# Head norm of a Taylor attention: sums for two groups at once, roots copied across partitions, values normed in place

## The chip, the cores and the metric

One core of one Trainium2 chip. The metric is the device time of one execution in microseconds (us). The engines are TensorE (PE; its weight loads are listed as PEld), VectorE (DVE), ScalarE (ACT), GpSimd (POOL) and SyncE (SP), which issues all of the DMA transfers of this kernel.

## The reference

The input x has 8 sequences (batches) of 512 tokens with 128 features. Two blocks are applied, each with a layer norm before, a layer norm after and a residual:

```
x = x + layernorm(taylor_attention(layernorm(x)))
x = x + layernorm(six_layer_transformer(layernorm(x)))
```

The first block is the one that changes. Its attention has 16 heads; a query or key has 16 features, a value has 64. The weight of a pair of tokens is a Taylor series of the exponential, which equals 0.5 * ((1 + q.k/4)^2 + 1), with a causal mask and no softmax. Behind it each head is normed on its own:

```
A   = tril(1 + s + s*s/2),  s = q.k/4
y   = A @ v                                            # per head, 512 x 64
y   = y * rsqrt(mean(y*y over 64) + 1e-5) * g_weight   # the head norm
out = concat(heads) @ Wo.T
```

The second block has six layers of local attention (window 32) and a gated feed-forward. It is unchanged, and it takes most of the time.

## The kernel before

The attention stage runs over groups of four heads: NQ = 4 groups in a batch, NG = 32 groups in all. Values are held transposed, with the 64 features of two heads in the 128 partitions and the 512 tokens along the row, so a group has a tile `yT` of 128 x 2 x 512, whose two halves hold two heads each.

A group takes three steps (`STEPS`), by blocks of keys: block 0, block 1, and blocks 2 and 3 together. `slot(k)` writes the order of PE for one step: `squares(k)` (scores `sc`, squared on ACT to `am`, masked on DVE at L283, which the text calls the keep), the head norm of an earlier group, the projections of the next group (`project_qk` in the second step, `project_v` in the third), the work of the neighbouring batches, and `weigh(k - 2)` (`y`, the weighted values, accumulated in PSUM). PE follows this order as written (`manual_schedule`); the order on the other engines is set by a scheduler, within the data dependencies. All engines are in order.

At the end of a group `weigh` lets DVE add the column sums `vs` to `y` and write `yT` (L308), and ACT square it to `ysq` (L313). The PSUM tile `y` has one buffer, so the next group's first `y` product waits for `yT`. Two slots after a group has ended, `head_norm(G)` computes the norm: PE multiplies `ysq` by `same` (128 x 128, ones in two 64 x 64 blocks), so that each partition gets the sum of its own head (L321); ACT takes the logarithm (L322) and exp(-0.5 * log) (L324), which gives the inverse root `rs` in each partition; DVE multiplies `yT`, the weight `gw` and `rs` to `yn` (L326). `attn_out(b)` multiplies the eight `yn` halves of a batch by Wo (`po`, L336), in the second group of the next batch, third step; a layer norm, a residual and a store of `x1` follow. The PSUM tiles of the tag `tr` (two buffers) serve `qk`, `vv`, `ms` and `po` in turn; the copies `tv` (L252) free those of `vv`.

The last pieces of this stage lie beside the first steps of the transformer: `head_norm(NG - 1)` at t = 0, and `attn_out(B - 1)` at t = 1.

Of the kernel before, what the change touches and what calls it, by code (L numbers as in the profile page):

```python
# [8 lines left out]
F32 = mybir.dt.float32  # L9
BF16 = mybir.dt.bfloat16  # L10
AF = mybir.ActivationFunctionType
ALU = mybir.AluOpType
# [3 lines left out]
P = 128  # L16
# [3 lines left out]
HD = 64  # L20
W = 32
# [7 lines left out]
def sandwich_kernel(ctx: ExitStack, tc: tile.TileContext, ins: dict, out: bass.AP):  # L29
    nc = tc.nc  # L30
    x_d = ins["L0_attn_hidden_states"]
    B, N, _ = x_d.shape
    NB = N // P
# [5 lines left out]
    NCH = len(CH)  # L39

    const = ctx.enter_context(tc.tile_pool(name="const", bufs=1))
# [23 lines left out]
    gw = vec[:, NV : NV + 1]  # L65
# [16 lines left out]
    tables, exps, divisions, copies, pcopies, maxima = [], [], [], [], [], []  # L82
# [12 lines left out]
    def issue_behind(later, earlier):  # L95
        tc.add_manual_dep(
            later.ins, earlier.ins.name,
            mybir.DependencyInfo(mybir.DependencyClass.NoSync, mybir.DependencyReason.DATA),
            reason="order on an engine",
        )  # L100
# [37 lines left out]
    psum = ctx.enter_context(tc.tile_pool(name="psum", bufs=2, space=PSUM))  # L138
    wl = ctx.enter_context(tc.tile_pool(name="wl", bufs=2))
    f2 = ctx.enter_context(tc.tile_pool(name="f2", bufs=2))  # L140
    f3 = ctx.enter_context(tc.tile_pool(name="f3", bufs=3))
    f1 = ctx.enter_context(tc.tile_pool(name="f1", bufs=1))
# [3 lines left out]
    NQ = H // 4  # L146
# [4 lines left out]
    def load_x(b):  # L151
        t = f2.tile([P, NP, W + P], F32, tag="kT", name=f"xin_{b}")
        xin[b] = t.rearrange("p a b -> p (a b)")[:, : NB * DM].rearrange("p (n d) -> p n d", d=DM)
        nc.sync.dma_start(xin[b], x_d[b].rearrange("(n p) d -> p n d", p=P))


    tw = wl.tile([P, 3, 2, 512], F32, tag="wqkv", name="tw")
    a_w = ins["attn_w"].rearrange("p (t s c) -> p t s c", t=3, s=2)
    nc.sync.dma_start(tw[:, 0], a_w[:, 0])
    load_x(0)  # L160
    nc.sync.dma_start(tw[:, 1], a_w[:, 1])
    nc.sync.dma_start(tw[:, 2], a_w[:, 2])
    nc.sync.dma_start(vec, ins["vectors"])
# [8 lines left out]
        out=keep, in_=keep, compare_op=ALU.is_ge, fill=0.0, base=0, pattern=[[1, P]], channel_multiplier=-1,  # L172
    )

    same = const.tile([P, P], F32, tag="same", name="same")
    nc.vector.memset(same, 0.0)
    for a in range(2):
        nc.vector.memset(same[HD * a : HD * (a + 1), HD * a : HD * (a + 1)], 1.0)
    eps4 = const.tile([P, 1], F32, tag="eps4", name="eps4")
    nc.vector.memset(eps4, 4.0 * EPS)  # L180

# [12 lines left out]
    for qd in range(4):  # L194
        r = slice(qd * W, (qd + 1) * W)
# [5 lines left out]
    NG = NQ * B  # L201
    bt = [dict() for _ in range(B)]
    gr = [dict() for _ in range(NG)]

    def norm_in(b):
        if b + 1 < B:
            load_x(b + 1)
        bt[b]["xl"] = xl = f1.tile([P, NB, DM], F32, tag="xn", name=f"xl_{b}")
        layer_norm(f2, xl, xin.pop(b), NB, by_log=True)
# [24 lines left out]
    def project_qk(G):  # L234
        b, g = divmod(G, NQ)
        gr[G]["qk"] = qk = f2.tile([P, 2, N], F32, tag="pe", name=f"tqk_{G}")
        for s in range(2):
            ps = psum.tile([P, N], F32, tag="tr", name="qk")
            nc.tensor.matmul(ps, wqk[:, s, g * P : (g + 1) * P], bt[b]["xlT"], start=True, stop=True)  # L239
            nc.scalar.copy(qk[:, s], ps)  # L240
# [48 lines left out]
    def weigh(k):  # L289

        G, s = steps[k]
        b, g = divmod(G, NQ)
        if s == 0:
            gr[G]["y"] = psum.tile([P, 2, N], F32, tag="s", name="y", bufs=1)
        y, v = gr[G]["y"], gr[G]["v"]
        am, places = gr[G].pop(("am", s))
        for m, o, n in places:
            for h in range(4):
                r = slice(HD * (h % 2), HD * (h % 2 + 1))
                nc.tensor.matmul(  # L300
                    y[r, h // 2, m * P :], v[:, m, h * HD : (h + 1) * HD], am[:, h, o : o + n],
                    start=(m == 0), stop=(m == NB - 1), skip_group_check=True,
                )
        if s == len(STEPS) - 1:
            yT = f2.tile([P, 2, NB, P], F32, tag="sq", name="yT")
            with tc.high_priority():
                for i in range(2):
                    nc.vector.tensor_tensor(  # L308
                        yT[:, i], y[:, i].rearrange("p (n m) -> p n m", m=P),
                        bt[b]["vs"][:, 2 * g + i, :].unsqueeze(2).to_broadcast([P, NB, P]), ALU.add,  # L310
                    )
            ysq = f2.tile([P, 2, N], F32, tag="t1", name="ysq")
            nc.scalar.activation(ysq, yT.rearrange("p a n m -> p a (n m)"), AF.Square)  # L313
            gr[G]["yT"], gr[G]["ysq"] = yT, ysq

    def head_norm(G):
        yT, ysq = gr[G].pop("yT"), gr[G].pop("ysq")
        rs = f2.tile([P, 2, N], F32, tag="t2", name="rs")
        for i in range(2):
            ps = psum.tile([P, N], F32, tag="tr", name="ms")  # L320
            nc.tensor.matmul(ps, same, ysq[:, i], start=True, stop=True)  # L321
            ln = nc.scalar.activation(rs[:, i], ps, AF.Ln, bias=eps4, scale=1.0 / HD)  # L322
            issue_behind(ln, tables[-1])
        exps.append(nc.scalar.activation(rs, rs, AF.Exp, scale=-0.5))  # L324
        gr[G]["yn"] = yn = f1.tile([P, 2, N], F32, tag=("qT", "pT", "on", "oT")[G % NQ], name="yn")
        nc.vector.scalar_tensor_tensor(  # L326
            yn.rearrange("p a n -> p (a n)"), yT.rearrange("p a n m -> p (a n m)"), gw,
            rs.rearrange("p a n -> p (a n)"), ALU.mult, ALU.mult,
        )

    def attn_out(b):

# [28 lines left out]
    def slot(k):  # L361

        G, ph = divmod(k, len(STEPS))
        b, g = divmod(G, NQ)
        if k < len(steps):
            squares(k)
        if ph == 0 and 0 <= G - 2 < NG:
            head_norm(G - 2)
        if ph == 1 and G + 1 < NG:
            project_qk(G + 1)  # L370
        if ph == 2 and G + 1 < NG:
            project_v(G + 1)
        if g == 0 and ph == 1 and b + 1 < B:
            norm_in(b + 1)
        if g == 1 and ph == 0 and b + 1 < B:
            in_by_features(b + 1)
        if g == 1 and ph == 1 and b + 1 < B:
            sums_before(b + 1)
        if g == 1 and ph == 2 and b >= 1 and k < len(steps):
            attn_out(b - 1)  # L380
        if g == 2 and ph == 2 and b >= 1 and k < len(steps):
            to_state(b - 1)
        if 0 <= k - 2 < len(steps):
            weigh(k - 2)
# [333 lines left out]
    def at(t, lag, step, *args, ends=False):  # L718
        if 0 <= t - lag < len(units) and (not ends or units[t - lag]["j"] == NB - 1):
            step(units[t - lag], *args)  # L720
# [3 lines left out]
    with tc.manual_schedule(engines={mybir.EngineType.PE}):  # L724
        norm_in(0)
        in_by_features(0)
        project_qk(0)
        project_v(0)
        sums_before(0)
        layers[0] = load_layer(0)  # L730
        for k in range(len(steps) + 2):
            slot(k)
        for t in range(len(units) + 7):
            if t < len(units):
                u = units[t]
                if u["l"] not in layers:
                    layers[u["l"]] = load_layer(u["l"])
                u["L"] = layers[u["l"]]


            gelus = 0 <= t - 5 < len(units) and units[t - 5]["j"] == NB - 1
            at(t, 0, proj, 0)
            at(t, 0, proj, 1)


            if t % NB == 1 and NB < t <= len(units) - NB * (B - 1):
                nc.tensor.addr_align(128, offset=IN_STEP)
            at(t, 2, by_keys)
            if gelus:
                gelu_only()  # L750
            at(t, 3, out_project)

            if t == 0:
                head_norm(NG - 1)
            if t == 1:
                attn_out(B - 1)
            at(t, 1, by_features, 0)
            at(t, 2, weigh_values)
            at(t, 1, by_features, 4, 0)
            at(t, 0, values)  # L760
            if t == 3:
                to_state(B - 1)
            at(t, 0, sum_squares, 0)
            at(t, 0, sum_squares, 1)
            if not gelus:
                at(t, 0, unit_length)
            at(t, 1, by_features, 4, 1)
            at(t, 0, spread)
            at(t, 3, feed_norm, ends=True)
            at(t, 4, feed_first, ends=True)  # L770
            at(t, 5, feed_middle, ends=True)
            if gelus:
                at(t, 0, unit_length)
            at(t, 6, feed_last, ends=True)
            at(t, 1, scores)
            at(t, 3, feed_normed, ends=True)
            at(t, 2, out_by_features)
# [91 lines left out]
```

## Time and profile before

| | |
|---|---|
| median of 3 runs | 3826.05 us |
| lowest and highest | 3818.64 and 3838.03 us |
| profiled execution, its own time | 3825.62 us |
| its span, first to last instruction | 3823.9 us |
| mean granted TensorE clock | 0.994 |
| PE busy in the span | 3703.6 us |
| DVE, ACT, POOL busy | 2794.7, 2662.9, 1842.6 us |
| stretch 100 to 500 us (attention): PE busy | 395.69 of 400 us |

A line of a group reads: line of the kernel, engine, operation, out<-in by the names of the tiles, the part of the array (for PE: rows * columns), shapes, count | busy time, mean ns of one | idle time of the engine just before, and what ended it. A float32 product is issued as two PE instructions, so counts on PE are twice those of the code. A line of a timeline has the start in us, the length, and the same names. In a table of stretches the DMA share is the mean busy share of the core's 16 DMA engines, and GB/s is what they moved.

### The profile page before, as it was taken

How to read it: one execution, taken by the hardware profiler on the slowest of the kernel's cores; microseconds unless marked ns; L12 is line 12 of the kernel's file. 1: busy time of each engine (PE TensorE's matmuls, PEld its weight loads, DVE VectorE, ACT ScalarE, POOL GpSimd, SP SyncE). 2: the span in 40 equal slices, each digit the busy share in tenths (PEclk: the TensorE clock that was granted, in tenths of full speed). 3: DMA queues.
4: the chain of work that ended last, by engine and by line, in shares of the span. 5: the costliest groups of instructions: out<-in, count | busy, mean ns of one | idle time of the engine just before them, and what ended most of it. 6: DMA issues, size and time to landing. Idle time of an engine off the chain costs nothing.

```text
span 3823.9 us, 152697 instructions
## 1 busy us (share of the span) xinstructions
PE 3703.6 (97%) x65600; PEld 2456.2 (64%) x65600; DVE 2794.7 (73%) x4308; ACT 2662.9 (70%) x6750; POOL 1842.6 (48%) x1311
## 2 busy tenths in 40 slices
PE   8999999999999999999999999999999999989997
PEld 4545556666666666666666666666666666666664
DVE  4555567787877778787777778777777878777774
ACT  5565557777777777777777777777777777767665
POOL 0000025555555555555555655555555555555552
PEclk9999999999999999999999999999999999999998
DMA  2000012222232222322222322223222222222221
GB/s 82 17 9 12 6 51 72 60 67 62 73 79 69 66 58 66 81 73 62 67 66 58 88 72 67 57 67 82 71 65 65 67 58 65 65 67 69 64 67 32
DMA packets 153219, 233.66 MB, mean 61 GB/s; under 512 B 32622, under 2 KB 53356, under 8 KB 151788
## 3 DMA queue, kind: packets, MB, share of 16 engines
q1 hardware_dynamic: 152556, 223.89, 22.8%
q8 instruction: 530, 8.68, 0.9%
q14 instruction: 133, 1.09, 0.1%
HBM read 24.54 MB, written 4.19 MB: 8 GB/s over the span
## 4 chain that ended last, share of the span: by engine, by line
PE 95%; issue 2%; ACT 2%; DVE 1%; POOL 0%; DMA 0%; POOLq 0%; SPq 0%; DVEq 0%; ACTq 0%
PE tr L79 20%; PE mm L439 17%; PE py L627 9%; PE mm L497 9%; PE po L598 8%; PE sp L558 8%; PE y L300 4%; PE mm L652 3%; PE mm L654 3%; PE py L687 3%; PE sc L270 3%; PE sp L551 2%; PE vv L248 2%; PE qk L239 1%; PE po L336 1%
## 5 line engine op out<-in xcount | busy, mean ns | idle before, releaser
L470 POOL TENSOR_TENSOR qk<-t,t 128x1024 f32<-128x1024 f32 x384 | 909.9, 2370 | 679.3 <-DVE t L454 405.3
L486 POOL TENSOR_TENSOR qk<-qk,ss 128x1024 f32<-128x1024 f32 x384 | 722.2, 1902 | 16.0
L439 PE MATMUL mm<-wqkv,state 128*128 128x512 f32 x1536 | 698.4, 597 | 2.6 <-ACT v L502 2.6
L447 DVE TENSOR_TENSOR t<-mm,tab 128x512 f32<-128x512 f32 x768 | 498.6, 671 | 239.5 <-PE mm L439 239.5
L570 ACT ACTIVATE pe<-sp,mx 128x64 f32<-128x64 f32 x3072 | 652.1, 381 | 2.3 <-DVE mx L566 2.3
L462 ACT ACTIVATE sq<-mm 128x512 f32<-128x512 f32 x768 | 421.3, 607 | 118.6 <-DVE t L454 114.0
L454 DVE TENSOR_TENSOR t<-mm,tab 128x1024 f32<-128x1024 f32 x384 | 468.4, 1220 | 5.9
L439 PEld LDWEIGHTS mm<-wqkv,state 128*128 128x128 f32 x1536 | 273.7, 191 | 289.6 <-issue 242.2
L473 DVE TENSOR_REDUCE ss<-sq 128x16 f32<-128x1024 f32 x384 | 448.6, 1209 | 0.7 <-ACT sq L462 0.6
L79 PE MATMUL tr<-ident,qk 128*128 128x128 f32 x3072 | 440.7, 276 | 1.8 <-ACT qT L536 0.8
L536 ACT COPY kT<-tr 128x512 f32<-128x512 f32 x384 | 225.6, 587 | 299.6 <-PE tr L79 299.4
L79 PEld LDWEIGHTS tr<-ident,qk 128*128 128x128 f32 x3072 | 351.0, 141 | 120.7 <-issue 100.8
L627 PE MATMUL py<-oT,wo 128*128 128x128 f32 x3072 | 377.4, 276 | 0.5 <-ACT oT L620 0.5
L627 PEld LDWEIGHTS py<-oT,wo 128*128 128x128 f32 x3072 | 364.5, 194 | 0.7 <-ACT oT L620 0.7
L497 PE MATMUL mm<-wqkv,state 128*128 128x512 f32 x768 | 363.1, 595 | 0.3 <-ACT sq L462 0.3
L620 ACT COPY oT<-tr 128x512 f32<-128x512 f32 x384 | 206.8, 589 | 221.5 <-PE tr L79 218.9
L598 PE MATMUL po<-v,pT 64*32 64x64 f32 x24576 | 301.9, 225 | 56.0 <-PE tr L79 49.1
L598 PEld LDWEIGHTS po<-v,pT 64*32 64x32 f32 x24576 | 274.2, 105 | 98.0 <-PE tr L79 88.5
L566 DVE TENSOR_REDUCE mx<-sp 128x16 f32<-128x1024 f32 x192 | 235.1, 1225 | 104.2 <-PE sp L558 104.2
L558 PE MATMUL sp<-kT,qT 64*32 64x64 f32 x24576 | 304.7, 226 | 6.4 <-issue 6.4
L558 PEld LDWEIGHTS sp<-kT,qT 64*32 64x32 f32 x24576 | 270.6, 105 | 62.5 <-issue 60.0
L606 DVE TENSOR_TENSOR on<-po,su 128x1024 f32<-128x1024 f32 x192 | 235.2, 1225 | 96.8 <-PE po L598 96.8
(114 smaller groups left out, 5082.8 us busy)
## 6 DMA issues: line engine op xcount, KB each, us to landing
v<-v SPq DMA_DIRECT2D x1152, 128.0 KB
v<-v SPq DMA_DIRECT2D x672, 64.0 KB
wqkv<-in_L_ffn_Wqkv_dram SPq DMA_DIRECT2D x6, 1536.0 KB
wo<-in_L_ffn_Wo_dram SPq DMA_DIRECT2D x6, 512.0 KB
xin<-_attn_hidden_states_dram SPq DMA_DIRECT2D x8, 256.0 KB
xr<-_attn_hidden_states_dram SPq DMA_DIRECT2D x8, 256.0 KB
x<-xr SPq DMA_DIRECT2D x8, 256.0 KB
xr<-x SPq DMA_DIRECT2D x8, 256.0 KB
```

Of the source, the lines that this page charges most:

```text
L79: nc.tensor.transpose(ps[:cols, :rows], src, ident[:rows, :rows])
L439: nc.tensor.matmul(ps[:, a].rearrange("p h d -> p (h d)"), lhs, wqkv[:, s, a, :], start=True, stop=True)
L447: nc.vector.tensor_tensor(t2[:, a], ps[:, 1 - a], tab[:, 2 * s + 1, j, HF * a : HF * (a + 1)].unsqueeze(1).to_broadcast([P, H, HF]), ALU.mult,
L454: nc.vector.tensor_tensor(t1, ps, tab[:, 2 * s, j, :].rearrange("p (a d) -> p a d", a=2).unsqueeze(2) .to_broadcast([P, 2, H, HF]), ALU.mult,)
L470: nc.gpsimd.tensor_tensor(qk[:, s].rearrange("p h a d -> p a h d"), t1, t2, ALU.add)
L473: su = nc.vector.tensor_reduce(u["ss"][:, s], u["sq", s].rearrange("p h a d -> p h (a d)"), AX.X, ALU.add)
L486: nc.gpsimd.tensor_tensor(t, t, ss[:, i, :].unsqueeze(2).to_broadcast([P, H, HD]), ALU.mult)
L497: nc.tensor.matmul(ps[:, p, :], lhs, L["wqkv"][:, 2, p, :], start=True, stop=True)
L558: nc.tensor.matmul(sp[W * w : W * (w + 1), p, pair, :], qT[HD * p : HD * (p + 1), pair, W * w : W * (w + 1)], kT[HD * p : HD * (p + 1), pa ...
L570: ex = nc.scalar.activation(pe[:, pair, p, :], sp[:, p, pair, :], AF.Exp, bias=mx[:, p, pair : pair + 1])
L598: nc.tensor.matmul(po[W * w : W * (w + 1), p, pair, :], pT[r, pair, W * w : W * (w + 1)], v2[r, w, HD * pair : HD * (pair + 1)], start=Tru ...
L627: nc.tensor.matmul(py, L["wo"][:, c, :], oT[:, c, :], start=(c == 0), stop=(c == NP - 1))
```

## The change

`head_norm` is called for two groups at once, in every second group, with the first of the two as its argument. The constant `same` becomes `of`, 128 x 32, with ones of one head in the even columns and of the other in the odd columns. Four products, one for each half of the two groups, write 32 partitions each of one PSUM tile `ps`: partition 32c + a holds the sum of head a of half c. ACT takes one logarithm and one exponential of 128 x 512, into a tile `rt` (tag `gT`). The eight rows that matter, one for each head, are then copied to the 64 partitions of their heads in `rs` by eight DMAs from SP, each with a source that is repeated 64 times. DVE multiplies in place: `yT` is both input and output, and is also what `attn_out` reads. `yT` now takes its buffer in turn from six places: the four single-buffer tags that `yn` had and the two buffers of `sq`.

The last call at t = 0 is for the last two groups. Apart from the head norm, the load of the first batch's x is issued ahead of the first third of the attention weights, where it was second.

```diff
     tw = wl.tile([P, 3, 2, 512], F32, tag="wqkv", name="tw")
     a_w = ins["attn_w"].rearrange("p (t s c) -> p t s c", t=3, s=2)
+    load_x(0)
     nc.sync.dma_start(tw[:, 0], a_w[:, 0])
-    load_x(0)
     nc.sync.dma_start(tw[:, 1], a_w[:, 1])
...
-    same = const.tile([P, P], F32, tag="same", name="same")
-    nc.vector.memset(same, 0.0)
+    of = const.tile([P, W], F32, tag="of", name="of")
+    nc.vector.memset(of, 0.0)
     for a in range(2):
-        nc.vector.memset(same[HD * a : HD * (a + 1), HD * a : HD * (a + 1)], 1.0)
+        nc.vector.memset(of[HD * a : HD * (a + 1), a::2], 1.0)
...
         if s == len(STEPS) - 1:
-            yT = f2.tile([P, 2, NB, P], F32, tag="sq", name="yT")
+            i = (G + 2) % (NQ + 2)
+            yT = (f1 if i < NQ else f2).tile(
+                [P, 2, NB, P], F32, tag=("qT", "pT", "on", "oT", "sq", "sq")[i], name="yT"
+            )
...
     def head_norm(G):
-        yT, ysq = gr[G].pop("yT"), gr[G].pop("ysq")
-        rs = f2.tile([P, 2, N], F32, tag="t2", name="rs")
-        for i in range(2):
-            ps = psum.tile([P, N], F32, tag="tr", name="ms")
-            nc.tensor.matmul(ps, same, ysq[:, i], start=True, stop=True)
-            ln = nc.scalar.activation(rs[:, i], ps, AF.Ln, bias=eps4, scale=1.0 / HD)
-            issue_behind(ln, tables[-1])
-        exps.append(nc.scalar.activation(rs, rs, AF.Exp, scale=-0.5))
-        gr[G]["yn"] = yn = f1.tile([P, 2, N], F32, tag=("qT", "pT", "on", "oT")[G % NQ], name="yn")
-        nc.vector.scalar_tensor_tensor(
-            yn.rearrange("p a n -> p (a n)"), yT.rearrange("p a n m -> p (a n m)"), gw,
-            rs.rearrange("p a n -> p (a n)"), ALU.mult, ALU.mult,
-        )
+        ps = psum.tile([P, N], F32, tag="tr", name="ms")
+        for c in range(4):
+            nc.tensor.matmul(
+                ps[W * c : W * (c + 1)], of, gr[G + c // 2]["ysq"][:, c % 2], start=True, stop=True,
+                skip_group_check=True,
+            )
+        rt = f1.tile([P, NCH, N], F32, tag="gT", name="rt")[:, 0]
+        ln = nc.scalar.activation(rt, ps, AF.Ln, bias=eps4, scale=1.0 / HD)
+        issue_behind(ln, tables[-1])
+        exps.append(nc.scalar.activation(rt, rt, AF.Exp, scale=-0.5))
+        for g in range(2):
+            rs = f2.tile([P, 2, N], F32, tag="t2", name="rs")
+            for i in range(2):
+                for a in range(2):
+                    r = W * (2 * g + i) + a
+                    nc.sync.dma_start(
+                        rs[HD * a : HD * (a + 1), i], rt[r : r + 1].unsqueeze(1).to_broadcast([1, HD, N])
+                    )
+            yT = gr[G + g]["yT"].rearrange("p a n m -> p (a n m)")
+            nc.vector.scalar_tensor_tensor(yT, yT, gw, rs.rearrange("p a n -> p (a n)"), ALU.mult, ALU.mult)
+            gr[G + g]["yn"] = gr[G + g]["yT"].rearrange("p a n m -> p a (n m)")
...
-        if ph == 0 and 0 <= G - 2 < NG:
-            head_norm(G - 2)
+        if ph == 0 and G % 2 and 0 <= G - 3 < NG:
+            head_norm(G - 3)
...
             if t == 0:
-                head_norm(NG - 1)
+                head_norm(NG - 2)
```

## Prediction

> **What bounds the kernel now.** I read the page first, for shares and the chain; then stretches of the attention stage; then the groups and one 13 us period of its timeline; last the DMA rates, because the change puts transfers where there are none. On the page:
>
> ```profile
> PE 3703.6 (97%) x65600; PEld 2456.2 (64%) x65600; DVE 2794.7 (73%) x4308; ACT 2662.9 (70%) x6750; POOL 1842.6 (48%) x1311
> PE 95%; issue 2%; ACT 2%; DVE 1%; POOL 0%; DMA 0%; POOLq 0%; SPq 0%; DVEq 0%; ACTq 0%
> ```
>
> TensorE is busy 97% of the span and carries 95% of the chain. The attention stage (its last head norm starts at 535.8) shows the same in a table of stretches, whose columns are PE, PEld, DVE, ACT and POOL busy, clock, DMA share and GB/s:
>
> ```profile
> 100.00:500.00 400.00, 395.69 (x2489) 213.53 (x2487) 209.57 (x458) 226.97 (x328) 7.92 (x7) 0.99 0.03 11
> ```
>
> PE 395.7 of 400 us, VectorE 210, ScalarE 227, the DMA engines at 3%. Time taken from PE is therefore gained, and time taken from ScalarE alone is not. The groups of the first 480 us show today's price of the part that changes:
>
> ```profile
> L321 PE MATMUL ms<-ysq,same 128*128 128x512 f32 x108 | 54.8, 623 | 0.1
> L322 ACT ACTIVATE rs<-ms,eps 128x512 f32<-128x512 f32 x54 | 34.7, 692 | 0.0
> L326 DVE SCALAR_TENSOR_TENSOR yn<-yT,vec,rs 128x1024 f32<-128x1024 f32 x27 | 34.7, 1284 | 24.0 <-ACT rs L324 23.9
> L324 ACT ACTIVATE rs<-rs 128x1024 f32<-128x1024 f32 x27 | 28.6, 1058 | 0.5
> ```
>
> One period on PE (start, length):
>
> ```profile
> 202.37 1.14 PE L270 MATMUL sc<-tqk 32*128 32x512 f32 x8
> 203.44 1.98 PE L321 MATMUL ms<-ysq,same 128*128 128x512 f32 x4
> 205.35 1.51 PE L300 MATMUL y<-am,tv 128*64 128x384 f32 x8
> 206.79 0.93 PE L270 MATMUL sc<-tqk 32*128 32x384 f32 x8
> 207.65 1.98 PE L239 MATMUL qk<-xlT,tw 128*128 128x512 f32 x4
> 209.56 1.52 PE L300 MATMUL y<-am,tv 128*64 128x256 f32 x16
> 211.01 0.94 PE L270 MATMUL sc<-tqk 32*128 32x256 f32 x16
> 211.88 1.99 PE L248 MATMUL vv<-tw,xlT 128*128 128x256 f32 x8
> ```
>
> From start to start: two full-array ms products take 1.91 us; four sc products on a quarter of the array each take 1.07, so quarters do run together. The next y (one accumulator bank pair) starts at 213.80, 10.36 after ms, and needs yT evacuated by VectorE; in every batch's second group po (L336) stands at this place and needs yn.
>
> **Part 1, the sums.** A pair of groups has two head norms now: 2 x 1.91 = 3.82. After, four 32-column products on four quarters: 1.07 like sc (bounds: 1.07, and 3.82 if quarters of columns queue; y, with 64 columns, does four products in 1.87, two at a time, so I take 1.07). Gain 2.75 a pair, 16 pairs: 44 us, all on PE. ScalarE drops from four logarithms and two exponentials (4 x 0.69 + 2 x 1.06 = 4.9) to one of each on 512 columns (0.69 + about 0.6 = 1.3); it was idle 43% of the stretch, so this counts for nothing. VectorE keeps its two products of 1.28 a pair; in place costs nothing that a row shows. The buffers that rotate over six places are last read by po at least four slots before they are written again: no wait.
>
> **Part 2, the spread.** Eight copies a pair, 128 copies in all. Each reads one partition's 2 KB 64 times and writes 64 partitions, 128 KB. The nearest rows are DMA stretches (length, clock, DMA share, GB/s): a weight load to 128 partitions, the x1 store from 128 partitions, and one copy between 32 and 32 partitions:
>
> ```profile
> 15.00:16.00 1.00, 1.00 1.01 423
> 243.40:244.30 0.90, 1.00 0.77 291
> 2015.25:2016.00 0.75, 1.00 0.37 87
> ```
>
> Rate over share over 16 is what one engine moves while busy: 26.2, 23.6 and 14.7 GB/s. With 32 partitions instead of 128 an engine is slowed to 56-62%: engines wait for each other at the partitions, at source or target, and two that share deliver 29.4 together. One source partition makes all 16 share. So from above I price a copy as if one engine did it: 131072 B at 26.2 GB/s is 5.0 us (4.46 at 29.4, 5.55 at 23.6). From below: if only the target counted, copies would follow each other as the 64-partition v copies do, about 0.6 us apart. I take 5.0, because the slowing grows as partitions fall from 128 to 32 and one is far beyond that; both ends are kept. The Trainium skill, "SBUF — State Buffer", section Door 1, says that DMA bandwidth depends on the ports that the partitions reach, that p and p+32 share a port, and measures 27.6 GB/s for partitions 0 to 3. By that a copy would be 4.75 us (an estimate), and the forecast below 32 us less.
>
> Who waits: the order of the changed kernel's VectorE has, in each pair: keep (L283), product g0, yT (two halves), product g1, tv copy, two keeps, tv copy. VectorE is in order, so yT waits behind g0's four copies and the tv copies behind all eight. With T0 the start of ms: the squares hold ScalarE to T0+2.0, logarithm and exponential to T0+3.35. The copy issued at 2014.28 moves its first bytes 1.2 us later, so bytes flow from about T0+4.7. At 5.0 each, g0 has landed at T0+24.7, g1 at T0+44.7.
>
> - Pairs without po (8): PE reaches y at 10.36 - 0.84 = T0+9.5. Product g0 ends at 26.0, yT at 27.3: 17.8 lost. PE runs y, sc, y, sc (1.87 + 1.07 + 1.44 + 0.86 = 5.2) to 32.5, where qk needs banks that the tv copies free; product g1 ends at 46.0, the first copy at 46.7: 14.2 lost; the second bank comes at 48.7, 1.0 after PE wants it. 33.0 lost, less 2.75: +30.3.
> - Pairs with po (7, and the last one, whose po at 546.13 comes 10.3 after its ms): PE waits at po from 9.5 to 46.0: 36.5, less 2.75: +33.8.
>
> Sum 8 x (30.3 + 33.8) = 513. After a stall PE may restart slowly: the first qk group of the run, after idle, took 3.63 against 1.98 (the page's clock is 0.50 for 6.5 us a little later). 24 restarts at 1.65 are 40 (bounds 0, and 24 x 3.25 = 78).
>
> Of SP's queue: x1's store, the xr and xin loads and the first v copies stand behind the spreads; each is wanted tens of us later or waits for the same stall, so nothing is added.
>
> **Part 3, the first load.** xin goes ahead of the 512 KB of tw. At 377 GB/s (3.00:6.00) that is 1.4 us, and its issue is 0.43 earlier; PE's first transposes wait for it. I take -1.5 (bounds -1.8 and 0).
>
> The sum stands against the profiled execution: 3825.6 us (span 3823.9 and 1.7 around it), 0.4 under the median of 3826.05. 3825.6 + 513 + 40 - 1.5 = **4377 us**. The price of a copy enters 16 x 8 = 128 times: 4.46 gives -69, 5.55 gives +70; with the restarts this case is 4268 to 4485.
>
> **The rivals.**
> - Two of the copies are served at once (another path per half of the array, packets of two rows mixed): 2.5 us a copy. g0 at T0+14.7, g1 at 24.7. Without po 7.8 + 4.2 + 1.0 - 2.75 = 10.3, with po 26.0 - 9.5 - 2.75 = 13.8; 8 x 24.1 = 193, restarts 20, load -1.5: 4037, within about 3990 to 4080.
> - The other side: the source partition costs nothing and only the target counts. For it: the 64-partition copies run 0.6 apart, and rereading q_scale's one line of DRAM at the start goes at 215 to 260 GB/s. Against it: that line is not on-chip memory, and no copy here has under 32 partitions at the source. g0 lands by T0+7, product g0 ends at 8.2, yT at 9.5, just in time; g1 lands at T0+9.6, its product ends at 10.9, and po waits 1.4 in eight pairs. 3825.6 - 44 - 1.5 + 11 = 3791. It decides below about 1.0 us a copy: there eight pairs with po lose what the sixteen gain (4.7 + 8 x 0.78 + 1.28 is 9.5 + 2.75).
> - The quarters of columns queue after all and the copies are cheap: the 44 is gone, 3835, no change. Beside slow copies this adds 44, within the range's top.
>
> **How the numbers follow.** A few runs tell about 0.5% (19 us) from no change. Chances: one copy at a time 0.66, two at once 0.14, slower still than 4490 0.02, cheap copies with the gain kept 0.15, nothing either way 0.03. So faster 0.15, same 0.03, slower 0.82. The first case alone is 4268 to 4485; range with the second 3990 to 4490, which leaves out the 0.02, 0.15 and 0.03.
>
> **What would show it.** In the profile after: ms of four 32-column products in about 1.1 us once per pair; the stretch of T0+5 to T0+45 with the DMA share near 1 at 25 to 30 GB/s; VectorE's product waiting about 20 us for a DMA twice per pair; PE's waits on yT, tv and the normed yT 15 to 37 us long, and PE near half busy to about 1050 us instead of 97% to 540. I am wrong if a spread's rate is above 150 GB/s, if the products at VectorE start within 5 us of the exponential, or if PE stays over 95% busy.

## The result, and the profile after

The changed kernel takes 4331.07 us (median of 4 runs, 4325.55 to 4335.27), against 3826.73 us for the kernel before in the same session: 1.1315 times as long (95% interval 1.1286 to 1.1343). The forecast was 4377 us, in a range of 3990 to 4490. The shares, the chain, and, in 40 equal slices of the span, PE's busy share and its granted clock (both in tenths) on the page of the changed kernel:

```profile
PE 3723.3 (86%) x65600; PEld 2470.1 (57%) x65600; DVE 2790.9 (64%) x4308; ACT 2614.5 (60%) x6686; POOL 1842.2 (43%) x1311
PE 79%; SPq 8%; DMA 6%; issue 2%; DVE 2%; ACT 2%; POOL 0%; POOLq 0%; DVEq 0%; ACTq 0%
PE   6554465454999999999999999999999999999997
PEclk8777777776999999999999999999999999999998
```

PE's busy time rose by 19.7 us and the span by 503.5: PE stood idle for 604 us where it had stood for 120. Nearly all of that rise, 480 of 484 us, lies in the first quarter of the span (to 1075 us), where the attention stage is. The chain has two new members, SP's queue (8%) and the DMAs (6%), which had 0% before. The same stretch as before, in the table of stretches (PE, PEld, DVE, ACT, POOL busy, clock, DMA share, GB/s):

```profile
100.00:500.00 400.00, 215.65 (x1308) 114.34 (x1312) 112.01 (x252) 102.44 (x151) 3.83 (x3) 0.75 0.50 22
```

PE is busy 215.65 us where it was busy 395.69, and the DMA engines are at 50% while they move 22 GB/s: busy, and delivering little. The chain of cause, from the list of waits of the first 1000 us (total, times, longest):

```profile
DVE yT L342 <- DMA rs<-rt: 497.0, 30, 19.0
PE po L350 <- DVE tv L252: 228.7, 7, 34.7
PE y L300 <- DVE yT L312: 125.2, 8, 17.8
PE qk L239 <- DVE tv L252: 63.4, 7, 9.7
```

VectorE waits 497 us for the copies; PE waits behind VectorE, for the evacuation `yT`, for `tv`, and for `tv` at `po`. One pair without po, on SP, VectorE and PE; its ms starts at 313.06 (T0):

```profile
316.37 27.03 SPq L338 DMA_DIRECT2D rs<-rt  x8
```

```profile
337.52 1.28 DVE L342 SCALAR_TENSOR_TENSOR yT<-yT,vec,rs 128x1024 f32<-128x1024 f32 x1 [18.83 <-DMA rs<-rt]
338.84 1.29 DVE L312 TENSOR_TENSOR yT<-y,vs 128x512 f32<-128x512 f32 x2
355.29 1.28 DVE L342 SCALAR_TENSOR_TENSOR yT<-yT,vec,rs 128x1024 f32<-128x1024 f32 x1 [15.16 <-DMA rs<-rt]
```

```profile
313.06 1.06 PE L325 MATMUL ms<-ysq,of 128*32 128x512 f32 x8
340.28 3.68 PE L300 MATMUL y<-am,tv 128*64 128x512 f32 x8 [17.70 <-DVE yT L312]
343.88 2.03 PE L270 MATMUL sc<-tqk 32*128 32x512 f32 x8
357.23 3.88 PE L239 MATMUL qk<-xlT,tw 128*128 128x512 f32 x4 [8.37 <-DVE tv L252]
```

The four sums take 1.06 us (the forecast said 1.07), so quarters of columns do run together. The roots of the first group have landed at T0+24.5, those of the second at T0+42.2. `y` waits 17.70 us and `qk` 8.37. After a stall PE runs at half clock (0.50 in the rows below): the eight `y` instructions take 3.68 us, where they took 1.94 at 310.12, before the stall. SP's queue is itself held for 27 us while it issues eight copies. The rate while the first group's copies run, and around the change to those of the second group:

```profile
326.00:330.00 4.00, 0.00 (x0) 0.00 (x0) 0.00 (x0) 0.00 (x0) 0.00 (x0) 0.50 0.89 27
334.00:338.00 4.00, 0.00 (x0) 0.00 (x0) 0.48 (x1) 0.00 (x0) 0.00 (x0) 0.50 0.92 40
```

16 engines, 89% busy, move 27 GB/s together. At 4.7 us a copy the first row holds the change from source row 1 to row 32 (at about 326.8), and nothing gets faster there, though copies of both rows can overlap. The second holds the change from row 33 to row 64 (about 336.2), and the rate rises to 40. What the engines share at the source therefore seems to reach over rows 0, 1, 32 and 33, and not to row 64.

### The profile page after: what moved, and what is told of

The parts are those of the page before. It is cut to its first block, busy times and chain, and to the rows that moved or that the text cites. A ratio compares the mean times of both kernels' runs of the same rounds, so it can differ in the third digit from the quotient of the medians.

```text
span 4327.4 us, 152965 instructions
## 1 busy us (share of the span) xinstructions
PE 3723.3 (86%) x65600; PEld 2470.1 (57%) x65600; DVE 2790.9 (64%) x4308; ACT 2614.5 (60%) x6686; POOL 1842.2 (43%) x1311
## 4 chain that ended last, share of the span: by engine, by line
PE 79%; SPq 8%; DMA 6%; issue 2%; DVE 2%; ACT 2%; POOL 0%; POOLq 0%; DVEq 0%; ACTq 0%
PE tr L79 18%; PE mm L453 15%; SPq L338 8%; PE py L641 8%; PE mm L511 8%; PE po L612 7%; PE sp L572 7%; DMA rs<-rt 6%; PE mm L666 3%; PE mm L668 3%; PE py L701 3%; PE sp L565 2%; PE po L350 2%; PE y L300 1%; PE qk L239 1%
## 5 line engine op out<-in xcount | busy, mean ns | idle before, releaser
L359 POOL TENSOR_TENSOR xr<-xr,ao 128x512 f32<-128x512 f32 x8 | 10.2, 1274 | 909.0 <-DVE ao L127 909.0
L342 DVE SCALAR_TENSOR_TENSOR yT<-yT,vec,rs 128x1024 f32<-128x1024 f32 x32 | 41.1, 1285 | 531.1 <-DMA rs<-rt 531.1
L300 PE MATMUL y<-am,tv 128*64 128x512 f32 (+3 forms) x1024 | 176.3, 480 | 156.9 <-DVE yT L312 125.2
```

## The experiments

The theory: one source partition sets the rate of a copy (4.7 us for 128 KB), and everything else follows from VectorE, which is in order. The rivals: the target or the issue sets the rate, or the waits in VectorE's order cost whatever the rate is. Two more questions came up on the way: where the 44 us of the shorter sums went, and whether the idea can be made to win. Ratios are against the kernel before, run on the same chip in the same call.

**One: more source rows.** `of` already makes 16 equal rows for each head (every second column of a quarter). Each copy reads 16 of them, each repeated four times. Nothing else differs.

```diff
-                        rs[HD * a : HD * (a + 1), i], rt[r : r + 1].unsqueeze(1).to_broadcast([1, HD, N])
+                        rs[HD * a : HD * (a + 1), i],
+                        rt[r : r + W - 1 : 2].unsqueeze(1).to_broadcast([HD // 4, 4, N]),
```

> The same eight copies of 128 KB to the same 64 partitions each, but from sixteen source partitions (every second one of the quarter, all of which hold the same root), each repeated 4 times, in place of one partition repeated 64 times. Source theory (one partition serves all 16 DMA engines at one engine's rate): a copy falls from 4.7 us to about 0.6, the products at VectorE no longer wait tens of us, PE returns to over 95% busy, and the time is about 3790 us (3778 to 3810). Target theory (the 64 written partitions or the repeated 2 KB reads set the rate): the copies stay near 4.7 us and the time near 4331. Order theory (the in-order waits of VectorE behind eight DMAs cost, whatever the rate): between 3826 and 4000.

Measured: 3838.15 us, ratio 1.0021 (1.0008 to 1.0033). Eight copies now take 5.3 us from their first byte to their last (at 197.74 and 203.07, first issue at 196.52; 5.3 to 6.8 in the sixteen pairs), where they took 37.3: 196 GB/s against 28. The row of this stretch, with columns as in the tables above:

```profile
197.74:203.07 5.33, 5.00 (x42) 3.15 (x40) 2.58 (x3) 1.38 (x3) 0.00 (x0) 1.00 0.86 196
```

Reading 16 rows instead of one takes away all but 8 of the 504 us, with the same targets, bytes and number of issues: the source is the cause of the slowdown. With more rows go fewer repeats of each (4 and not 64), and no run changes one without the other; but if the repeat of one row were the cause, the change from row 1 to row 32 above should have been faster too. The kernel doesn't get below the one before, though, as it should have: 3838 misses the 3778 to 3810 of the source theory and lies in the range of the order theory. The next experiment looks for what is missing.

**Two: no copies at all.** The products read the tile of roots as it stands, so the norm uses the roots of other heads; the spread is left out.

```diff
+        rs = rt.unsqueeze(1).to_broadcast([P, 2, N])
         for g in range(2):
-            rs = f2.tile([P, 2, N], F32, tag="t2", name="rs")
...
-            nc.vector.scalar_tensor_tensor(yT, yT, gw, rs.rearrange("p a n -> p (a n)"), ALU.mult, ALU.mult)
+            y3 = gr[G + g]["yT"].rearrange("p a n m -> p a (n m)")
+            nc.vector.scalar_tensor_tensor(y3, y3, gw, rs, ALU.mult, ALU.mult)
```

> The spread is left out: both groups' products read the tile of roots directly (128 x 512, the same for each half), so the norm is by the wrong roots. What stays is the quarter sums, the single logarithm and exponential, the product in place and the earlier first load. My sum for these parts alone: 3826 - 44 - 1.5 = 3780 us. If the product in place or the rotation of yT's buffers costs something, it shows here: above 3790.

Measured: 3824.24 us, ratio 0.9984 (0.9974 to 0.9993). With the sums in 1.06 us and the copies free, 6 us are gained and not 46. The waits of PE in this kernel, from 100 to 500 us:

```profile
PE sc L270 <- ACT am L279: 12.8, 7, 1.8
PE vs L230 <- ACT tqk L240: 3.7, 5, 0.7
```

In the kernel before, the same list has, beside 0.8 us at `vs`, one line:

```profile
PE tr L79 <- ACT rs L322: 3.4, 5, 0.7
```

The place of the longer wait, on PE and on ACT:

```profile
240.43 1.36 PE L270 MATMUL sc<-tqk 32*128 32x384 f32 x4 [1.84 <-ACT am L279]
241.73 3.19 PE L239 MATMUL qk<-xlT,tw 128*128 128x512 f32 x4
```

```profile
239.17 0.30 ACT L104 ACTIVATE ln_rs<-ln_mv,eps 128x4 f32<-128x4 f32 x1 [1.80 <-DVE ln_mv L117]
239.37 1.00 ACT L279 ACTIVATE am<-sc 128x1024 f32<-128x1024 f32 x1
```

In the third group of each batch, ACT's square `am` stands in its queue behind the logarithm of attn_out's second layer norm, which waits 1.80 us for VectorE. Before, PE had the even group's 1.91 us of sums to do in that time; now that is gone, and PE waits 1.84 for `am`. A second wait, at `vs`, grows from 0.16 to 0.74 us, while that of 0.69 at `tr` is gone. Behind each of these waits the clock falls (columns as above):

```profile
239.00:240.00 1.00, 0.00 (x0) 0.00 (x0) 1.00 (x10) 0.83 (x2) 0.00 (x0) 1.00 0.49 191
240.00:241.00 1.00, 0.57 (x4) 0.30 (x4) 0.76 (x4) 0.97 (x5) 0.00 (x0) 0.88 0.00 0
241.00:242.00 1.00, 1.00 (x5) 0.28 (x2) 1.00 (x5) 0.76 (x2) 0.00 (x0) 0.50 0.00 0
242.00:243.00 1.00, 1.00 (x2) 0.48 (x3) 1.00 (x5) 0.65 (x1) 0.00 (x0) 0.50 0.00 0
243.00:244.00 1.00, 1.00 (x2) 0.42 (x2) 0.76 (x2) 0.16 (x1) 0.00 (x0) 0.50 0.54 151
244.00:245.00 1.00, 1.00 (x4) 0.16 (x4) 0.00 (x0) 0.48 (x2) 0.00 (x0) 0.91 0.68 185
```

From 240.8 to 244.2 the clock is 0.50, so one such window costs 1.7 us. Between 60 and 470 us there are 12 waits and 13 windows, against 2 windows in the kernel before. That is the hypothesis to test: waits of 12.8 + 3.7 = 16.5 us, less the 4.2 of the kernel before, and 11 windows more x 1.7 = 19 us, together some 31 of the 40 us that are missing. The expectation named another cause for a time above 3790, the product in place or the rotation of `yT`'s buffers; the experiment on the uncovered waits, below, keeps both.

**Three: 16 rows side by side.** As the first experiment, but the ones of `of` fill adjacent columns, so a copy reads 16 neighbouring rows.

```diff
-        nc.vector.memset(of[HD * a : HD * (a + 1), a::2], 1.0)
+        nc.vector.memset(of[HD * a : HD * (a + 1), W // 2 * a : W // 2 * (a + 1)], 1.0)
...
-                        rt[r : r + W - 1 : 2].unsqueeze(1).to_broadcast([HD // 4, 4, N]),
+                        rt[r : r + W // 2].unsqueeze(1).to_broadcast([HD // 4, 4, N]),
```

> As with sixteen source partitions, but sixteen adjacent ones (the sum matrix has its ones in columns 0 to 15 for one head and 16 to 31 for the other). If a source partition is limited by itself, this is the same as every second of 32: about 3790 us, and a copy takes 0.6 us. If partitions share doors by fours (the Trainium skill, SBUF - State Buffer, section Door 1: partitions 4n to 4n+3 and those 32 further share a port), sixteen adjacent ones reach four doors instead of eight, and a copy takes about 1.2 us: the eight pairs with po lose about 3.4 us each and the eight others about 2.6, together 3825 to 3840 us.

Measured: 3851.61 us, ratio 1.0061 (1.0044 to 1.0079), 12 us above the range. One packet of 2 KB in ten takes 307 ns or more, against 166 ns with rows two apart, and the last of eight copies lands 7.4 to 8.4 us after the first issue instead of 6.5 to 8.0 (sixteen pairs). So neighbouring rows are slower, as they would be if they share a way out of the memory, but a copy does not take twice as long. The 13 us over the first experiment are less than the 35 to 50 that were expected over 3790; the range was missed because the start was not 3790 but 3838. Why the copies slow down so little is not shown.

**Four: the slow copies, unread.** The copies from one row as in the changed kernel, but the products read `rt` as in the second experiment, so VectorE doesn't wait for the copies.

```diff
-            nc.vector.scalar_tensor_tensor(yT, yT, gw, rs.rearrange("p a n -> p (a n)"), ALU.mult, ALU.mult)
+            y3 = gr[G + g]["yT"].rearrange("p a n m -> p a (n m)")
+            r2 = rt.unsqueeze(1).to_broadcast([P, 2, N])
+            nc.vector.scalar_tensor_tensor(y3, y3, gw, r2, ALU.mult, ALU.mult)
```

> The copies from one partition are made as in the change, but the products read the tile of roots directly (wrong roots), so no engine waits for a copy but the next pair's logarithm, which must not overwrite the roots before they are copied. Source theory: the copies still take about 37.6 us a pair, one pair's logarithm to the next is then at least 0.7 + 0.6 + 1.2 + 37.6 = 40 us where PE needs 30, so the 16 pairs lose about 10 each and the time is 3900 to 3980 us: of the 551 us that the spread costs, roughly 150 are the rate and 400 the waits at VectorE. Order theory: 3780 to 3800 us, since nothing at VectorE waits.

Measured: 4136.39 us, ratio 1.0801 (1.0785 to 1.0817), 156 us above the top of what was expected. What the expectation overlooked is that the copies still hold their source: `ao` of attn_out has the buffer of `rt` (tag `gT`), and so has the next pair's `rt`. The waits of the first 1000 us show both, each ended by the landing of the copies:

```profile
ACT rt L330 <- DMA rs<-rt: 104.5, 6, 25.7
DVE ao L127 <- DMA rs<-rt: 101.6, 5, 23.6
```

So a slow copy with no reader at all still costs 312 us over the kernel without copies; that VectorE reads the copies accounts for the other 195 or so.

**Five: four copies from 32 rows.** With adjacent ones in `of`, a quarter's 32 rows are what one target of 128 partitions needs.

```diff
-                for a in range(2):
-                    r = W * (2 * g + i) + a
...
+                r = W * (2 * g + i)
+                nc.sync.dma_start(rs[:, i], rt[r : r + W].unsqueeze(1).to_broadcast([W, P // W, N]))
```

> The spread from 32 source rows: the ones of `of` fill columns 0 to 15 for the first head of a pair and 16 to 31 for the second, so a quarter's 32 rows hold the 32 copies that one 128-partition target needs, and four copies of 256 KB take the place of eight of 128 KB. Theory (the number of source partitions sets the rate, and the copies' issues and their fixed latency the rest): the two copies of the first group land about 4.5 us and those of the second about 5.5 us after the first issue, against 6.6 for the last of eight copies with 16 rows; pairs with po wait about 1 us instead of 0.4 to 3.2. About 3830 us (3820 to 3840), 0.2% below the kernel with 16 strided rows. Rival (neighbouring rows share a way out of the memory and the bytes per copy are double): each copy takes as long as two of the adjacent 16-row kernel, the last lands at 8 us or later, 3845 to 3860 us.

Measured: 3896.32 us, ratio 1.0176 (1.0161 to 1.0191), above the ranges of theory and rival alike. The copies are hardly slower: the last byte comes 6.84 us after the first issue (210.48 and 217.32). The order of VectorE is what differs. This kernel, and then the first experiment:

```profile
215.71 1.28 DVE L339 SCALAR_TENSOR_TENSOR yT<-yT,vec,rs 128x1024 f32<-128x1024 f32 x1 [5.77 <-DMA rs<-rt]
217.81 1.28 DVE L339 SCALAR_TENSOR_TENSOR yT<-yT,vec,rs 128x1024 f32<-128x1024 f32 x1 [0.21 <-DMA rs<-rt]
219.13 1.29 DVE L312 TENSOR_TENSOR yT<-y,vs 128x512 f32<-128x512 f32 x2
```

```profile
201.15 1.28 DVE L343 SCALAR_TENSOR_TENSOR yT<-yT,vec,rs 128x1024 f32<-128x1024 f32 x1 [2.29 <-DMA rs<-rt]
202.46 1.29 DVE L312 TENSOR_TENSOR yT<-y,vs 128x512 f32<-128x512 f32 x2
203.67 1.28 DVE L343 SCALAR_TENSOR_TENSOR yT<-yT,vec,rs 128x1024 f32<-128x1024 f32 x1
```

With four copies the scheduler puts the evacuation `yT` behind both products, with eight between them. `y` on PE then waits 3.9 to 4.9 us in the pairs without po instead of 1.1 to 2.8. So this run says nothing clean about 32 rows; what it shows is that the place of `yT` in VectorE's queue, and the later landing of the first group, cost PE more than the last byte tells.

**Is the lost gain due to the uncovered waits?** The kernel without copies, with two moves: attn_out's second layer norm is issued in the next batch's third group, its logarithm behind that slot's last square; `sums_before` goes to the end of its slot. Beside it the control, the same two moves in the kernel before.

```diff
+    def state_norm(b):
...
+        layer_norm(f2, xs, bt[b].pop("xr"), NB, by_log=True, root=gr[0]["square"])
...
+        if g == 2 and ph == 0 and b >= 1 and k < len(steps):
+            state_norm(b - 1)
         if 0 <= k - 2 < len(steps):
             weigh(k - 2)
+        if g == 1 and ph == 1 and b + 1 < B:
+            sums_before(b + 1)
```

> The kernel without any spread (products read the roots of the quarters directly, so the norm is by other heads' roots, and the eight copies are left out), with two moves: the second layer norm of attn_out is issued in the next batch's third group, its logarithm behind that slot's last square, and sums_before of the next batch goes to the end of its slot, behind weigh. Theory (the 44 us that the quarter sums save were lost to two waits of TensorE per batch, 1.84 us for a square held behind the layer norm's logarithm and 0.74 us for a copy, and to 3.5 to 4 us of half clock after each): both waits are gone, the clock of 100 to 500 us is 0.98 or more, and the kernel takes about 3785 us (3775 to 3800), 37 below the kernel without the moves. Rival (the granted clock falls by itself, by how much work TensorE has done, and the waits only coincide with it): the waits go but the clock stays at 0.93 to 0.97, 3810 to 3824 us. Second rival (another engine then ends last in the same place): new waits of the same length at another tile, 3815 to 3830 us.

> The kernel before with the two moves alone (second layer norm in the next batch's third group, sums_before at the end of its slot). Control: if the moves are worth something only because the shorter sums uncovered the waits, nothing changes, 3820 to 3828 us (before's own wait of 0.69 us per batch for rs may go, at most 7 times about 2 us). Rival (the moves alone are the gain, whatever the sums): 3785 to 3800 us.

Measured: 3783.6 us, ratio 0.9883 (0.9869 to 0.9896), and the control 3828.4 us, ratio 0.9995 (0.9984 to 1.0007). The stretch of the first, in the table of stretches:

```profile
100.00:500.00 400.00, 394.47 (x2649) 212.78 (x2648) 235.41 (x509) 210.73 (x309) 15.92 (x12) 0.99 0.04 13
```

Both waits are gone, the clock is 0.99 with 2 half-clock windows between 60 and 470 us as in the kernel before, and the gain is there: 1.17% of 3829 are 45 us, against 44 and the 1.5 of the first load. The same moves without the shorter sums give nothing. So the gain of the sums was real, and it was lost to two waits, 2.6 us a batch together, and to the clock behind them; the product in place and the rotating buffers show no cost.

**Moving the head norm a slot ahead.** The full computation with the spread from 32 rows, both moves, and the whole of a pair's head norm one slot earlier (some 4 us on PE).

```diff
-        if ph == 0 and G % 2 and 0 <= G - 3 < NG:
-            head_norm(G - 3)
+        if ph == 2 and G % 2 == 0 and 0 <= G - 2 < NG:
+            head_norm(G - 2)
```

> Quarter sums with the full and right spread from 32 source rows, both moves of the layer norm and of sums_before, and the pair's head norm one slot earlier (behind the value projection's slot of the odd group), so that the copies have a slot more before the products are due. Theory: the copies are hidden and the gain of the sums arrives, about 3790 us (3780 to 3805), 1% below the kernel before. Rival: the copies in flight or VectorE's order behind them still hold TensorE about 1 us in each pair, and each such hold brings the half clock: 3815 to 3835 us, no change from before.

Measured: 3847.78 us, ratio 1.0054 (1.0040 to 1.0067): the rival, and 13 us above its range. VectorE meets the first product earlier too, and stands there for the copies:

```profile
223.15 1.28 DVE L341 SCALAR_TENSOR_TENSOR yT<-yT,vec,rs 128x1024 f32<-128x1024 f32 x1 [5.00 <-DMA rs<-rt]
```

```profile
227.42 1.58 PE L241 MATMUL qk<-xlT,tw 128*128 128x512 f32 x2 [4.30 <-DVE cb L223]
```

`cb` of the next batch stands behind the products on VectorE, and PE waits 4.30 us for it, once a batch.

**The head norm cut in two.** Sums, roots and copies stay a slot earlier; the two products are called at the changed kernel's place. Once with eight copies from 16 strided rows, once with four from 32 rows, and once with 16 rows but without the two moves.

```diff
+    def head_scale(G):
+        for g in range(2):
+            yT, rs = gr[G + g]["yT"].rearrange("p a n m -> p (a n m)"), gr[G + g].pop("rs")
+            nc.vector.scalar_tensor_tensor(yT, yT, gw, rs.rearrange("p a n -> p (a n)"), ALU.mult, ALU.mult)
...
+        if ph == 0 and G % 2 and 0 <= G - 3 < NG:
+            head_scale(G - 3)
```

> The full computation: quarter sums, a spread by eight copies from 16 strided rows each, both moves (second layer norm in the next batch's third group, sums_before at the end of its slot), and the head norm of a pair cut in two: sums, roots and copies one slot earlier (about 4 us before the changed kernel's place), the two products at VectorE left where the change has them. Theory (the early kernel lost because VectorE, in order, stood 5.0 us at the first product for the copies, with TensorE behind it for 4.3 us): the copies have landed 2 us before VectorE comes to the first product, no TensorE wait over 1 us is left in the attention stage, and the kernel takes the time of the kernel without a spread, 3785 us (3775 to 3800), 1.1% below before. Rival (the copies' traffic, or the issue of eight copies on SP, holds something else in each batch, each hold followed by half clock): 3810 to 3835 us.

> The same with four copies of 256 KB from 32 adjacent rows each in the place of eight from 16 strided rows. Their last bytes came 6.9 us after the first issue against 6.6 with strided rows, but the first group's came 5.2 us after it against about 4.6. Theory (with the products later than the copies, the order in which copies land no longer matters): as the kernel with strided rows within 0.3%, 3780 to 3800 us. Rival (the first group's copies are still late by the time VectorE comes): 1 to 3 us per pair and the half clock behind it, 3815 to 3850 us.

> The changed kernel with copies from 16 strided rows and the head norm cut in two, but without the two moves. Theory (the two waits of TensorE per batch that the shorter sums uncovered, and the half clock after them, cost the gain by themselves): as the kernel that has no spread at all, 3824 us (3815 to 3832), no change from before. Rival (the waits for the copies are the only loss): 3785 to 3800 us.

Measured: 3820.53 us (ratio 0.9980, 0.9971 to 0.9990), 3845.42 (1.0054, 1.0041 to 1.0066) and 3843.2 (1.0043, 1.0030 to 1.0056). All three miss their theory; the first two lie in the ranges of their rivals, the third above both of its ranges. The moves are worth 23 us here, and eight copies from strided rows 25 over four from adjacent ones. Cutting the function in two did not move the products: the scheduler still put them at VectorE as early as before, so it waited there for the DMAs (the strided kernel, second group of a batch):

```profile
211.36 1.28 DVE L349 SCALAR_TENSOR_TENSOR yT<-yT,vec,rs 128x1024 f32<-128x1024 f32 x1 [4.04 <-DMA rs<-rt]
```

The waits of PE that follow from it, and one of `xs` for the sums' PSUM buffer, from 100 to 500 us:

```profile
PE qk L241 <- DVE cb L223: 8.3, 5, 2.5
PE tr L79 <- ACT rt L332: 6.3, 7, 0.9
```

**The products tied to a place.** Each product is ordered behind the instruction that it must not hold up (the `yT` of the next group in a batch's second group, the last `tv` copy in its fourth), and `to_state` is a slot later.

```diff
+            issue_behind(scale, gr[0]["behind"])
...
-        if g == 2 and ph == 2 and b >= 1 and k < len(steps):
+        if g == 3 and ph == 0 and b >= 1 and k < len(steps):
             to_state(b - 1)
+        if ph == 2 and g == 3 and 0 <= G - 3 < NG:
+            head_scale(G - 3)
...
+        if ph == 1 and g == 1 and 0 <= G - 3 < NG:
+            head_scale(G - 3)
```

> The kernel with the head norm cut in two, 16 strided source rows and both moves (3820), with the pair's two products at VectorE put behind the next group's evacuation of y (even pairs) or behind the next tv copy (odd pairs), some 5 to 10 us later, and to_state one slot later, away from the sums' bank. Theory (what is left of the loss is VectorE in order: it waits 2.7 to 4.0 us at the first product, TensorE then waits 1.5 us for cb behind it, and 0.93 us for xs behind the sums' bank, each with the half clock after it): no wait over 1 us is left at TensorE between 100 and 500 us, the clock of that stretch is 0.98, and the kernel comes to the time without any spread, 3784 us (3778 to 3800), 1.1% below before. Rival (the copies' traffic of 46 GB/s or their issue on SP holds TensorE by itself): no gain, 3812 to 3825 us.

Measured: 3799.66 us against 3834.91 for the kernel before in that call, ratio 0.9908 (0.9891 to 0.9925). The full computation is now 0.9% faster than before, with the spread by DMA in it. The time is at the upper end of the theory's range, and "no wait over 1 us" didn't come true. Its stretch and what is left of PE's waits in it:

```profile
100.00:500.00 400.00, 390.53 (x2646) 209.31 (x2644) 224.59 (x503) 208.41 (x302) 10.27 (x10) 1.00 0.19 46
```

```profile
PE po L358 <- DVE tv L254: 7.9, 6, 1.6
```

The DMA engines move 46 GB/s at 19%, as in the kernel cut in two, and no wait of PE in this list is for them: the rival, traffic or issue by itself, does not hold. Two edits were made together here, the tie and the move of `to_state`; no run separates them. Against the kernel before in its own call this kernel gains 35 us and the one without copies 45. Of the 10 us or so between them, 9 are seven waits of 1.26 to 1.59 us at `po`, for `tv`, which stands behind the two products.

## Why the prediction was right

**The rate, and with it the sign.** A copy from one partition was taken as 5.0 us (bounds 4.46 and 5.55 in that case); the eight measured took 37.3 us from first byte to last, 4.7 each. The step to one source partition was argued from the slowing between 128 and 32 partitions, and the first experiment shows that the source does it. The Trainium skill, "SBUF — State Buffer", section Door 1, with its 27.6 GB/s, gave 4.75 for the copy, and the stretch above shows 27 GB/s. The page was nearer than my row.

**The stalls.** Forecast in pairs without po 17.8, 14.2 and 1.0; measured 17.6 to 17.8, 8.3 to 9.7 and none. Forecast at po 36.5; measured 32.2 to 32.4, once 34.7. The second stall, in the pair shown, is 5.8 us shorter because g1 landed 2.5 us earlier than forecast and because PE came to it later: `y`, `sc` and `sc` ran at half clock and took 7.2 us where I had 3.8 for them at full clock. The wait at po is 4 us shorter. It ends 1.5 us earlier: the second group lands some 2 us earlier, but po waits for the `tv` copy behind the product, 0.7 us more. And it starts at T0+12.2, not 9.5: I had overlooked that the next batch's transposes and `vs`, 2.5 us, lie in that slot. Stalls summed to 556 us in the forecast and PE's idle time rose by 484.

**The restarts.** 40 us were forecast with a top of 78. PE's busy time rose by 19.7 though the sums gave 44 back, so work at half clock cost about 64. I counted one slow `qk` group for each restart, and the clock stays at 0.50 for longer than that (the row that I read as 6.5 us lasts 6.8). The two misses, -72 and +24, partly cancel, which is luck; they leave the sum of the steps 48 us high, and the page's 4.75 us would have taken 32 of them.

**The sums and the first load.** Quarters run together: 1.06 us against 1.07. The first `qk` came 1.6 us earlier (forecast 1.5).

**The rivals.** The other side, "the source partition costs nothing", had the price 3791 us. The first experiment comes near its condition, with copies landing 6.6 us after the first issue, and took 3838. So this rival's price was wrong, and the step of it that failed is the gain of Part 1, 44 us "all on PE": without the copies it came to 6. PE at 97% doesn't mean that no engine stands close behind: the even group's 1.91 us covered an ACT queue that was 1.84 us late. Taking PE work away from such a place gave nothing there, and the clock took some more. For the same reason "this counts for nothing" was too quick on ScalarE: idle 43% on average, it was late in this one place. The sum behind "below about 1.0 us a copy" is also off: 0.78 is the price at which one pair with po loses its own 2.75, and not what sixteen gain.

## What to carry to other kernels

Before spreading rows by DMA, count the source partitions: if an array product writes the row, it may write many equal rows in the same time (here 32 rows in 1.06 us), and a copy can read many of them. When time is taken from a busy engine, look up what ran beside it on the others, and check that each wait it covered is still covered; a control with only the new order tells the two apart. Where a scheduler decides the order of an in-order engine, tie an instruction that waits for a DMA behind those that must not wait with it.

## What the runs showed of the hardware

The clock of PE fell to 0.50 for windows of 3.4 us, which cost 1.7 us each, after waits as short as 0.74 us: in the kernel without copies 12 waits of 0.74 to 1.84 us and 13 windows between 60 and 470 us. Their starts lie whole multiples of 3.41 us apart (90.58, 111.06 and 155.43 are the first three). The Trainium skill, "TensorE: Matmul & The Clock Gate", section What's actually happening, gives a free-running window of 3.4 us, which agrees with this length; the rule in its section HAM oscillation, no PE-idle gaps above about 3.4 us, does not cover waits this short. Nor does the length of a wait decide it: the kernel tied last had seven waits of 1.26 to 1.59 us in the same stretch and no window, the one cut in two (16 strided rows, both moves) had twelve of 0.86 to 2.47 us and one window, and the kernel before had two windows with waits of 0.69 alone. Two kernels in one stretch, without copies first and cut in two second:

```profile
100.00:500.00 400.00, 383.46 (x2487) 205.88 (x2486) 210.78 (x480) 195.21 (x287) 9.23 (x8) 0.95 0.04 11
```

```profile
100.00:500.00 400.00, 383.92 (x2561) 205.74 (x2562) 216.41 (x491) 205.02 (x297) 9.24 (x8) 1.00 0.19 46
```

PE is idle for the same 16 us in both, and the clock is 0.95 in one and 1.00 in the other. The kernel cut in two without the moves has much the same waits at `qk` and `tr`, and six of 1.8 us at `sc` besides; it has 18 windows between 60 and 470 us:

```profile
100.00:500.00 400.00, 375.47 (x2362) 201.97 (x2361) 198.63 (x447) 187.34 (x270) 7.95 (x7) 0.93 0.16 40
```

That the waits ahead of `vs` lie beside products of four columns could be a reason, but the waits of 1.8 us at `sc` don't, and a window comes with each of them in the kernel without copies. No run tells it, and it stays open.

One row as the source held 16 DMA engines to 27 GB/s, 16 rows two apart gave 196, and the issuing queue of SP was held for 27 us by eight copies of one row, against 5.0 to 6.6 with 16 rows.
